# A two-layer graph attention kernel: one more slot in layer 1's ring of rows, no transfers for missing edges, another order of the tiles

## The chip, the core and the metric

The kernel runs on one core of one Trainium2 chip. A core has five engines with instruction streams of their own: TensorE (PE in the profile; its weight loads are PEld), VectorE (DVE), ScalarE (ACT), GpSimd (POOL) and SyncE (SP). SP and ACT issue plain DMAs. POOL issues the indirect ones, which read or write a row per partition at an index taken from memory. Sixteen DMA engines move the bytes of all of them. The metric is the time of one execution on the device in microseconds. Before the change the median of three runs is 5479.6 us (5479.25 to 5485.96).

## The reference

There are 10,000 nodes with 768 numbers each, 160,000 random directed edges (80,000 pairs, both ways) and 10,000 self-loops. A node has 17 incoming edges on average. Two graph attention layers follow each other, cut here to what matters:

```python
def gat_conv(x, W, a_src, a_dst, bias, heads, out_ch, concat):
    xl = (x @ W).reshape(n, heads, out_ch)
    alpha_src, alpha_dst = einsum(xl, a_src), einsum(xl, a_dst)     # one number per node and head
    e = leaky_relu(alpha_src[src] + alpha_dst[dst], 0.2)
    e = exp(e - segment_max(e, dst)[dst])
    alpha = e / (segment_sum(e, dst)[dst] + 1e-16)
    return segment_sum(xl[src] * alpha, dst) + bias                  # the sum over a node's edges

h = gat_conv(x, W1, ..., heads=4, out_ch=256, concat=True)           # 1024 numbers a node
h = relu(layer_norm(h)) + (x @ Wr1 + br1)
h1 = h
h = gat_conv(h, W2, ..., heads=1, out_ch=768, concat=False)          # 768 numbers a node
h = layer_norm(h) + (h1 @ Wr2 + br2)
out = layer_norm(x + h)
```

## The kernel before

**Tables.** For each layer the kernel writes a table with a row per node: the transformed features, then the node's source and destination logits. A row of `table1` has 1,033 numbers (4,132 bytes): 1,024 features, 4 source and 4 destination logits, and the node's rank (below) in the last column. A row of `table2` has 770 numbers (3,080 bytes). Both tables have a row more, number `NP`, for missing edges: its features are 0 and its logits are -1e30, so that its weight comes out as 0; in `table1` its rank is `NP` itself.

**First stage** (lines 591 to 660). A loop over the 79 tiles of 128 nodes computes `x @ W1` on PE and the logits on DVE and ACT, adds the bias on POOL and writes `table1`. Beside it `prepare` (line 188) finds each node's edges and sorts the nodes by degree: the rank is a node's place in that order. Tile `t` of the sorted nodes gets `SLOTS[t]` slots, a bound on the degree of its nodes: 41 for tile 0, 27, 26, 25, 24, 24 for the next, 17 for tiles 36 to 43, 9 for tile 77 and 8 for tile 78; 1,377 in all. `slots` holds, for each partition and slot, the row to fetch; a slot without an edge holds `NP`. Slot 0 of a tile is the node's own row.

**The order of the tiles.** `TURNS` (line 96) gives the order in which both layers go through the tiles: 78, 76, ..., 2, 0, then 1, 3, ..., 77. So the numbers of slots rise from 8 to 41 and fall to 9.

**The ring** (`Ring`, line 434). A layer's gathered rows lie in a ring of `RING1` = 28 or `RING2` = 38 slots, 128 rows each. `ring.fetch` issues, on POOL, one indirect DMA per slot (line 418, through `gather`), in order; the gather of slot q + 28 is issued in the program after the work on slot q and waits for the engines that read it. In layer 2 a tile's own rows (slot 0) come by a plain DMA on SP instead, as the table lies in sorted order.

**Layer 1** (`ordered_layer1`, line 668). For each tile: `logits` (line 461) computes the weights of all its slots on DVE, with the exponential on ACT, and then copies the ranks from the last column of the fetched rows into `slots` (line 478, ACT), since layer 2's table lies in sorted order and its gathers need ranks. `normalised` divides the weights by their sum. The first one to four slots are added up on PE with diagonal matrices (lines 703 and 709). Of the others, each fourth is multiplied and added on DVE, head by head (line 508, four operations); the rest are multiplied by their weights on ACT (line 497) and added by DVE (line 504). Beside it PE transposes x and multiplies it by Wr1, and transposes the tile before, h, and multiplies it by W2. The weights of the next tile are begun when three slots of this one are left (`LEAD`), if `SLOTS[t + 1] + LEAD` is no more than the ring; so DVE then needs all rows of the next tile. A tile with more slots than the ring goes through `attend_parts` (line 511).

**x in layer 1.** `fetch_x` (line 677) gathers the tile's rows of x (384 KB) into one of two buffers. The rows of tile t + 2 are asked for at the end of tile t.

**Layer 2** (`ordered_layer2`, line 814) has the same shape with one head of 768: 512 columns are weighted on DVE (line 508), 256 on PE (line 860). PE also computes the residual (lines 871 and 874) from h1 and x. The result is scattered to the node's place by an indirect DMA on POOL with a bound (line 893): indices of nodes that don't exist are skipped.

```python
nc.gpsimd.indirect_dma_start(out=out, out_offset=bass.IndirectOffsetOnAxis(ap=nodes(t), axis=0),
                             in_=o, in_offset=None, bounds_check=N - 1, oob_is_err=False)
```

The order of the instructions on each engine is the order of the program (`tc.manual_schedule()`). `general_path` is for inputs that don't fit the slots; it doesn't run here.

Of the kernel before, what the change touches and what calls it, by code (L numbers as in the profile page):

```python
# [42 lines left out]
SCATTERS = 6  # L43
LISTS = 4
G = 4
RING1 = 28
RING2 = 38
LEAD = 3
DIAGONALS = 5
# [29 lines left out]
def gnn_kernel(ctx, tc, x, x_cols, src, dst, src_col, dst_col, W1, a_src1, a_dst1, b1, g1, be1, Wr1, br1,  # L79
               W2, a_src2, a_dst2, b2, g2, be2, Wr2, br2, out, n_edges):  # L80
    nc = tc.nc
    N, D0 = out.shape
    H1, DH1 = a_src1.shape
# [9 lines left out]
    CAPS = slot_counts(N, n_edges)  # L93
    SLOTS = CAPS

    TURNS = list(range(NT - 1, -1, -2))
    TURNS += sorted(set(range(NT)) - set(TURNS))
    FIRST, TOTAL = [0] * NT, 0
    for t in TURNS:
# [88 lines left out]
    def prepare():  # L188

        with tc.tile_pool(name="prep", bufs=1, side="right") as pool, \  # L190
# [107 lines left out]
                base, s = more, 2 * s  # L298
            nc.vector.tensor_sub(base, base, each)
            rank = pool.tile([P, NT], F32, name="rank")  # L300
            to = pool.tile([P, NT], I32, name="to")
            written = 0

# [33 lines left out]
            with nc.allow_non_contiguous_dma(reason="16 bytes a node"):  # L337
                for to, d in zip([sorted_] + others, order_d):
                    nc.sync.dma_start(to, d.rearrange("(t p) f -> p t f", p=P))
                    yield  # L340
                nc.sync.dma_start(table1[:NP, R1 - 1:].rearrange("(p j) r -> p (j r)", p=P), rank)
                yield
            for other in others:
                nc.vector.tensor_add(sorted_, sorted_, other)
# [72 lines left out]
    def gather(to, table, index, **more):  # L417
        nc.gpsimd.indirect_dma_start(out=to, out_offset=None, in_=table,  # L418
                                     in_offset=bass.IndirectOffsetOnAxis(ap=index, axis=0), **more)
# [14 lines left out]
    class Ring:  # L434

        def __init__(self, pool, table, row, size, own):
            self.table, self.size, self.own, self.issued = table, size, own, 0
            self.rows = pool.tile([P, size, row], F32, name="ring")  # L440

        def fetch(self, upto):
            for q in range(self.issued, min(upto, TOTAL)):
                if q in self.own:
                    nc.sync.dma_start(self.slot(q), self.table[self.own[q] * P:(self.own[q] + 1) * P, :])
                else:
                    gather(self.slot(q), self.table[:, :], slots[:, q:q + 1])
                self.issued = q + 1

        def slot(self, q):  # L450
# [10 lines left out]
    def logits(small, ring, lo, hi, ad, heads, c, top=None):  # L461


        n = hi - lo
        e = small.tile([P, ring.size, heads], F32, name="e")[:, :n]
        for a, b, rows in ring.parts(lo, hi):
            nc.vector.tensor_tensor(e[:, a - lo:b - lo], rows[:, :, c:c + heads],
                                    ad[:, None, :].to_broadcast([P, b - a, heads]), op=OP.add)
        leaky(e, e)
        new = small.tile([P, heads], F32, name="new")  # L470
        nc.vector.reduce_max(new, e.rearrange("p k h -> p h k"), axis=AX.X)
        if top is not None:
            nc.vector.tensor_max(new, new, top)
        nc.vector.tensor_tensor(e, e, new[:, None, :].to_broadcast([P, n, heads]), op=OP.subtract)  # L474
        nc.scalar.activation(e, e, AF.Exp)  # L475
        if not ring.own:
            for a, b, rows in ring.parts(lo, hi):
                nc.scalar.copy(slots[:, a:b], rows[:, :, R1 - 1])
        return e, new

    def normalised(small, e, heads, t):
# [109 lines left out]
    with tc.tile_pool(name="w1", bufs=1) as w1p, tc.tile_pool(name="l1", bufs=2) as io, \  # L591
# [14 lines left out]
        none = w1p.tile([P, R1], F32, name="none")[:1]  # L606
        nc.vector.memset(none[:, :C1], 0.0)
        nc.vector.memset(none[:, C1:], -BIG)
        nc.vector.memset(none[:, R1 - 1:], float(NP))
        nc.scalar.dma_start(table1[NP:NP + 1, :], none)  # L610
        nc.scalar.dma_start(table2[NP:NP + 1, :], none[:, C1 - C2:C1 + 2 * H2])

# [4 lines left out]
        def weight_steps():  # L617

            with nc.allow_non_contiguous_dma(reason="1024 numbers"):
                nc.scalar.dma_start(br1_c, br1.rearrange("(k p) -> p k", p=P))
            yield
            yield
            brT = spread_br1(w1p, "brT")
            load(w2, W2)
            for i, a in enumerate((a_src2, a_dst2)):
                vec = spread(w1p, a, "a2")
                for k in range(K1):
                    yield  # L630
                    m = io.tile([P, C1], F32, name="scr")[:, :C2]
                    nc.vector.tensor_mul(m, w2[:, k, :C2], vec)
                    nc.scalar.activation(m, m, AF.Copy, accum_out=w2[:, k, C2 + i:C2 + i + 1])
            load(wr1, Wr1)
            yield
            q = product(brT, w2, R2)
            row = io.tile([P, R1], F32, name="row")
            nc.scalar.copy(row[:, :R2], q[:, :R2])
            nc.vector.tensor_add(lift, row[:, C2:C2 + 1], row[:, C2 + 1:R2])
            nc.scalar.dma_start(shift, row[0:1, :C2])  # L640
# [3 lines left out]
        for t in range(NT):  # L644
            p = product(xTs.pop(t), w1, C1)
            row = io.tile([P, R1], F32, name="row")
            nc.scalar.copy(row[:, :C1], p[:, :C1])  # L647
            for i, vec in enumerate((as_b, ad_b)):
                m = io.tile([P, C1], F32, name="scr")
                nc.vector.tensor_mul(m, p[:, :C1], vec)  # L650
                for h in range(H1):
                    s = slice(h * DH1, (h + 1) * DH1)
                    nc.scalar.activation(m[:, s], m[:, s], AF.Copy,
                                         accum_out=row[:, C1 + i * H1 + h:C1 + i * H1 + h + 1])
            nc.gpsimd.tensor_add(row[:, :C1], row[:, :C1], b1_b)  # L655
            load_x(t + 2)
            nc.sync.dma_start(table1[t * P:(t + 1) * P, :R1 - 1], row[:, :R1 - 1])
            next(steps, None)
# [9 lines left out]
    def ordered_layer1():  # L668
        nonlocal ps_big
        with tc.tile_pool(name="b1", bufs=1) as pool, tc.tile_pool(name="small1", bufs=2) as small, \  # L670
# [4 lines left out]
            ring.fetch(SLOTS[0])  # L675

            def fetch_x(t):
                xt = pool.tile([P, D0], F32, name="xt", bufs=2)
                gather(xt, x[:, :], nodes(t))
                return xt  # L680

            xs = {t: fetch_x(t) for t in range(min(2, NT))}
            ring.fetch(RING1)
            g1_b, be1_b = (spread(pool, v, n) for v, n in ((g1, "g1"), (be1, "be1")))

# [5 lines left out]
            def weights_of(t):  # L691

                n, m = SLOTS[t], on_pe(t)
                e, _ = logits(small, ring, FIRST[t], FIRST[t] + n, ring.slot(FIRST[t])[:, C1 + H1:C1 + 2 * H1], H1, C1)
                yield e
                normalised(small, e, H1, t)

# [34 lines left out]
            for t in range(NT + 1):  # L732
# [24 lines left out]
                moves = []  # L757
                if live:
                    xT = pool.tile([P, K0, P], F32, name="xT")
                    moves = columns(xT, xs[t])  # L760
                multiplied(first + 2)
                if last:
                    h = pool.tile([P, C1], F32, name="h")
# [16 lines left out]
                if last:  # L780
                    events.append((first + 2, to_layer2))

                def due(k):
                    while events and events[0][0] <= k:
                        events.pop(0)[1]()

                if live and not whole:
                    due(n)
                    acc = ps_acc.tile([P, 2 * BANK], F32, name="acc")
                    ad = small.tile([P, H1], F32, name="ad")  # L790
                    nc.vector.tensor_copy(ad, ring.slot(FIRST[t])[:, C1 + H1:C1 + 2 * H1])
                    attend_parts(small, ring, acc, acc, ad, None, H1, DH1, t)
                ready = []
                ahead = iter(())
# [12 lines left out]
                last = None  # L807
                if live:
                    last = r, acc
                    if t + 2 < NT:  # L810
                        xs[t + 2] = fetch_x(t + 2)
            store(NT - 1)

    def ordered_layer2():
        nonlocal ps_big
        with tc.tile_pool(name="b2", bufs=1) as pool, tc.tile_pool(name="small2", bufs=2) as small, \
# [28 lines left out]
            def weights_of(t):  # L845
# [1 line left out]

                n = SLOTS[t]
                ad = small.tile([P, H2], F32, name="ad")
                nc.vector.tensor_add(ad, ring.slot(FIRST[t])[:, C2 + H2:], lift)  # L850
# [53 lines left out]
            for t in range(NT):  # L904
# [4 lines left out]
                if not whole(t):  # L909
                    for _ in last:  # L910
                        pass
                    ad = small.tile([P, H2], F32, name="ad")
                    nc.vector.tensor_add(ad, ring.slot(FIRST[t])[:, C2 + H2:], lift)
# [34 lines left out]
    def general_path():  # L948
# [82 lines left out]
        def attend_chunks(keep, work, small, lists, table, row, heads, dh, t):  # L1031
# [7 lines left out]
            nc.vector.tensor_copy(top, acc[:, c:c + heads])  # L1039
# [3 lines left out]
            nc.vector.tensor_copy(adm[:, :heads], acc[:, c + heads:c + 2 * heads])  # L1043
# [7 lines left out]
            with tc.For_i(lo, hi, G) as i:  # L1051
# [19 lines left out]
                for g in range(0, G, zg):  # L1071
                    z = work.tile([P, zg, heads, P], F32, name="z")
                    nc.vector.tensor_tensor(
                        z, off[:, g:g + zg, None, :].to_broadcast([P, zg, heads, P]),
                        xg[:, g:g + zg, c:c + heads, None].to_broadcast([P, zg, heads, P]), op=OP.add)
# [22 lines left out]
                nc.vector.tensor_add(e, xg[:, :, c:c + heads], sel[:, :, :heads])  # L1098
# [118 lines left out]
```

## Time and profile before

| what | value |
|---|---|
| median of three runs | 5479.6 us |
| the profiled execution | 5488.77 us, span 5487.0 us, mean granted clock 0.938 |
| PE, PEld | 4754.0 us (87%), 2827.1 us (52%) |
| DVE | 4328.8 us (79%) |
| ACT | 3148.0 us (57%) |
| POOL | 3247.4 us (59%) |
| DMA | 1581.74 MB, mean 288 GB/s |
| ring gathers, both layers (L418) | 2,675, mean 969 ns on POOL |

The first layer's gathers begin at 905 us and the second layer's at 3488 us. Times in the profile are in us unless ns is said. A line of the timeline gives the start, the length, the engine, the line of the kernel, the operation, what it writes and reads, and in brackets how long the engine had stood idle before it and what ended that. A busy share is a mean over stages that have different limits, so each stage is looked at by itself.

### The profile page before, as it was taken

The page shows a single profiled execution, that of the slowest core. Times are in us where ns is not written, and L with a number is a line of the kernel's source. Part 1 is how long each engine was busy: PE and PEld are TensorE (multiplying, and loading weights), DVE is VectorE, ACT ScalarE, POOL GpSimd, SP SyncE. Part 2 cuts the span into 40 slices and gives each one's busy share as a digit, 9 for nine tenths or more (in the row PEclk, how much of TensorE's full clock was granted, in tenths as well). Part 3 has the DMA queues.
Part 4 walks back from the last instruction along what each step waited for, and adds up shares of the span by engine and source line. Part 5 has one row for each costly group of instructions (what it writes and reads, how often), then busy time and mean ns, then how long its engine had stood idle before and what let it go on. Part 6 is the DMA issues. An engine that isn't in the chain of part 4 may idle for free. (4 is left out here: it accounts for less than half of the span.)

```text
span 5487.0 us, 58297 instructions
## 1 busy us (share of the span) xinstructions
PE 4754.0 (87%) x15032; PEld 2827.1 (52%) x15032; DVE 4328.8 (79%) x7766; ACT 3148.0 (57%) x8255; POOL 3247.4 (59%) x3238
## 2 busy tenths in 40 slices
PE   8999997999999875478999999799988746888998
PEld 3444443555555543245555555466655524555665
DVE  5784244899998888788999999498877786778998
ACT  3433344788888877678888888244433312333444
POOL 2445455455566555455665554377777775777774
PEclk9999998999999988789999999899998877899999
DMA  4333625899999988789999997699999987999996
GB/s 152 124 95 82 94 91 202 316 328 339 339 361 347 344 303 301 285 315 345 353 359 347 341 329 263 239 340 360 345 333 321 336 297 258 331 323 349 349 355 240
DMA packets 457866, 1581.74 MB, mean 288 GB/s; under 512 B 111851, under 2 KB 116011, under 8 KB 457526
## 3 DMA queue, kind: packets, MB, share of 16 engines
q0 software_dynamic: 328704, 1339.21, 68.3%
q1 hardware_dynamic: 126768, 235.29, 13.1%
q10 hardware_dynamic: 2054, 3.42, 0.2%
q8 instruction: 126, 2.06, 0.2%
q14 instruction: 214, 1.75, 0.1%
HBM read 1431.80 MB, written 146.23 MB: 288 GB/s over the span
## 5 line engine op out<-in xcount | busy, mean ns | idle before, releaser
L418 POOL DMA_INDIRECT ring<-table,slots x2675 | 2591.7, 969 | 1635.6 <-DVE acc L508 402.4
L508 DVE SCALAR_TENSOR_TENSOR acc<-ring,e,acc 128x256 f32<-128x256 f32 (+1 forms) x2538 | 1572.0, 619 | 127.5 <-PE acc L709 52.0
L497 ACT ACTIVATE ring<-ring,e 128x256 f32<-128x256 f32 x3320 | 1351.0, 505 | 0.0
L504 DVE TENSOR_TENSOR acc<-acc,ring 128x1024 f32<-128x1024 f32 x830 | 1022.5, 1232 | 72.8 <-ACT ring L497 1.2
L874 PE MATMUL big<-wr,w 128*128 128x512 f32 (+1 forms) x2528 | 857.9, 493 | 0.0
L169 PE MATMUL big<-w,xT 128*128 128x512 f32 x1896 | 827.7, 598 | 28.9 <-DMA w<-in_W_dram 11.2
L169 PE MATMUL big<-wr,xT 128*128 128x512 f32 x1896 | 834.1, 596 | 0.7 <-ACT xT L575 0.7
L169 PE MATMUL big<-w,hT 128*128 128x512 f32 (+1 forms) x2528 | 832.1, 486 | 1.2 <-ACT hT L575 1.2
L860 PE MATMUL big<-ring,diagonals 128*128 128x256 f32 x2672 | 660.8, 409 | 185.3 <-ACT diagonals L859 177.0
L860 PEld LDWEIGHTS big<-ring,diagonals 128*128 128x128 f32 x2672 | 543.6, 206 | 299.4 <-ACT diagonals L859 201.2
L169 PEld LDWEIGHTS big<-w,hT 128*128 128x128 f32 x2528 | 478.4, 189 | 375.0 <-issue 341.3
L709 PE MATMUL acc<-ring,diagonals 128*128 128x256 f32 x1816 | 456.6, 409 | 247.9 <-ACT diagonals L703 216.5
L874 PEld LDWEIGHTS big<-wr,w 128*128 128x128 f32 x2528 | 488.1, 193 | 350.3 <-issue 317.7
L169 PEld LDWEIGHTS big<-w,xT 128*128 128x128 f32 x1896 | 362.7, 192 | 491.9 <-issue 472.8
L169 PEld LDWEIGHTS big<-wr,xT 128*128 128x128 f32 x1896 | 356.9, 192 | 421.2 <-issue 420.3
L709 PEld LDWEIGHTS acc<-ring,diagonals 128*128 128x128 f32 x1816 | 370.1, 206 | 326.8 <-ACT diagonals L703 235.7
L859 ACT ACTIVATE diagonals<-ident,e 128x128 f32<-128x128 f32 x1336 | 399.6, 387 | 155.6 <-DVE e L488 117.9
L554 ACT ACTIVATE sd<-mv,eps 128x1 f32<-128x1 f32 x237 | 69.8, 294 | 614.0 <-DVE mv L552 613.6
L650 DVE TENSOR_TENSOR scr<-big,as_b 128x1024 f32<-128x1024 f32 x79 | 96.8, 1225 | 391.9 <-ACT row L647 391.9
L655 POOL TENSOR_TENSOR row<-row,none 128x1024 f32<-128x1024 f32 x79 | 187.2, 2369 | 280.5 <-ACT row L647 279.9
L703 ACT ACTIVATE diagonals<-ident,e 128x128 f32<-128x128 f32 x908 | 278.5, 387 | 96.4 <-DVE e L488 96.4
L475 ACT ACT_TABLE_LOAD x153 | 196.3, 1283 | 233.1 <-DVE e L474 205.9
(172 smaller groups left out, 3895.5 us busy)
## 6 DMA issues: line engine op xcount, KB each, us to landing
ring<-table,slots POOLq DMA_INDIRECT x2675, 6.5
table<-row SPq DMA_DIRECT2D x79, 516.0 KB, 3.6
h_d<-hT SPq DMA_DIRECT2D x79, 512.0 KB, 7.2
w<-h_d SPq DMA_DIRECT2D x79, 512.0 KB, 8.4
table<-row SPq DMA_DIRECT2D x79, 385.0 KB, 6.2
ring<-table SPq DMA_DIRECT2D x79, 385.0 KB, 6.5
xT<-in_x_cols_dram SPq DMA_DIRECT2D x79, 384.0 KB, 4.5
wr<-in_Wr_dram SPq DMA_DIRECT2D x2, 3072.0 KB
```

Source lines behind the costliest of these rows:

```text
L169: nc.tensor.matmul(p[:, c:e], aT[:, j, :], w[:, j, c:e], start=(j == 0), stop=(j == k - 1))
L418: nc.gpsimd.indirect_dma_start(out=to, out_offset=None, in_=table, in_offset=bass.IndirectOffsetOnAxis(ap=index, axis=0), **more)
L475: nc.scalar.activation(e, e, AF.Exp)
L497: nc.scalar.activation(row[:, s], row[:, s], AF.Copy, scale=e[:, h:h + 1])
L504: nc.vector.tensor_add(acc[:, :c], acc[:, :c], row[:, :c])
L508: nc.vector.scalar_tensor_tensor(acc[:, s], row[:, s], e[:, h:h + 1], (acc if first is None else first)[:, s], op0=OP.mult, op1=OP.add)
L655: nc.gpsimd.tensor_add(row[:, :C1], row[:, :C1], b1_b)
L703: nc.scalar.activation(diagonals[:, k * H1 + i, :], ident, AF.Copy, scale=e[:, k, i:i + 1])
L709: nc.tensor.matmul(acc[:, c:d], diagonals[:, k * H1 + i, :], ring.slot(FIRST[t] + k)[:, c:d], start=(k == 0 and c % BANK == 0), stop=(k == ...
L859: nc.scalar.activation(diagonals[:, k % G, :], ident, AF.Copy, scale=e[:, k, :])
L860: nc.tensor.matmul(to, diagonals[:, k % G, :], ring.slot(FIRST[t] + k)[:, ON_PE2:C2], start=False, stop=(k == n - 1), skip_group_check=True)
L874: nc.tensor.matmul(r[:, c:d], hT[:, j, :], wr2[:, j, c:d], start=False, stop=(j == K1 - 1 and (d < C2 or not whole(t))), skip_group_check= ...
```

## The change

Four things change.

1. `RING1` is 29 instead of 28. x in layer 1 has one buffer instead of two; the gather of tile t + 1's x is issued in the course of tile t, after two slots past those on PE, instead of x of tile t + 2 at the end of tile t.
2. Gathers from the second turn of the ring on carry `bounds_check=NP - 1`: an index of `NP` fetches nothing, and the slot keeps what was there. So that what was there has no weight, `logits` now writes -1e30 into the source logits of the slots that it has just read. For this the two kinds of logits change places in the tables' rows, destination first, and `table1` holds the negated rank in its last column: the same memset covers it, and `slots` becomes the smaller of the negated column and `NP`.
3. The copy of the ranks into `slots` moves from ACT to DVE, as that multiplication with minimum; the memset is on DVE as well, in both layers.
4. `TURNS` is 78, 77, ..., 48, then 47, 45, ..., 1, then 0, 2, ..., 46. The numbers of slots are 8 to 16 in the first 31 tiles, rise to 41 and fall to 16.

```diff
-RING1 = 28
+RING1 = 29
-    TURNS = list(range(NT - 1, -1, -2))
+    TURNS = list(range(NT - 1, NT * 3 // 5, -1)) + list(range(NT * 3 // 5, -1, -2))
     TURNS += sorted(set(range(NT)) - set(TURNS))
...
-                nc.sync.dma_start(table1[:NP, R1 - 1:].rearrange("(p j) r -> p (j r)", p=P), rank)
+                nc.vector.tensor_scalar(less_rank, rank, -1.0, None, op0=OP.mult)
+                nc.sync.dma_start(table1[:NP, R1 - 1:].rearrange("(p j) r -> p (j r)", p=P), less_rank)
...
                 if q in self.own:
                     nc.sync.dma_start(self.slot(q), self.table[self.own[q] * P:(self.own[q] + 1) * P, :])
+                elif q < self.size:
+                    gather(self.slot(q), self.table[:, :], slots[:, q:q + 1])
                 else:
-                    gather(self.slot(q), self.table[:, :], slots[:, q:q + 1])
+                    gather(self.slot(q), self.table[:, :], slots[:, q:q + 1], bounds_check=NP - 1,
+                           oob_is_err=False)
...
-            nc.vector.tensor_tensor(e[:, a - lo:b - lo], rows[:, :, c:c + heads],
+            nc.vector.tensor_tensor(e[:, a - lo:b - lo], rows[:, :, c + heads:c + 2 * heads],
                                     ad[:, None, :].to_broadcast([P, b - a, heads]), op=OP.add)
...
         nc.scalar.activation(e, e, AF.Exp)
-        if not ring.own:
-            for a, b, rows in ring.parts(lo, hi):
-                nc.scalar.copy(slots[:, a:b], rows[:, :, R1 - 1])
+        for a, b, rows in ring.parts(lo, hi):
+            if not ring.own:
+                nc.vector.tensor_scalar(slots[:, a:b], rows[:, :, R1 - 1], -1.0, float(NP), op0=OP.mult, op1=OP.min)
+            nc.vector.memset(rows[:, :, c + heads:], -BIG)
         return e, new
...
             def fetch_x(t):
-                xt = pool.tile([P, D0], F32, name="xt", bufs=2)
+                xt = pool.tile([P, D0], F32, name="xt")
                 gather(xt, x[:, :], nodes(t))
                 return xt
 
-            xs = {t: fetch_x(t) for t in range(min(2, NT))}
+            xt = fetch_x(0)
             ring.fetch(RING1)
...
+                def next_x():
+                    nonlocal xt
+                    xt = fetch_x(t + 1)
+
+                if t + 1 < NT:
+                    events.append((first + 2, next_x))
...
                     last = r, acc
-                    if t + 2 < NT:
-                        xs[t + 2] = fetch_x(t + 2)
```

More of the change, by code (lines that the diff above doesn't have):

```diff
@@ L300, in prepare @@
             rank = pool.tile([P, NT], F32, name="rank")
+            less_rank = pool.tile([P, NT], F32, name="less_rank")
             to = pool.tile([P, NT], I32, name="to")
@@ L608, in gnn_kernel @@
         nc.vector.memset(none[:, C1:], -BIG)
-        nc.vector.memset(none[:, R1 - 1:], float(NP))
         nc.scalar.dma_start(table1[NP:NP + 1, :], none)
@@ L626, in weight_steps @@
             load(w2, W2)
-            for i, a in enumerate((a_src2, a_dst2)):
+            for i, a in enumerate((a_dst2, a_src2)):
                 vec = spread(w1p, a, "a2")
@@ L647, in gnn_kernel @@
             nc.scalar.copy(row[:, :C1], p[:, :C1])
-            for i, vec in enumerate((as_b, ad_b)):
+            for i, vec in enumerate((ad_b, as_b)):
                 m = io.tile([P, C1], F32, name="scr")
@@ L693, in weights_of @@
                 n, m = SLOTS[t], on_pe(t)
-                e, _ = logits(small, ring, FIRST[t], FIRST[t] + n, ring.slot(FIRST[t])[:, C1 + H1:C1 + 2 * H1], H1, C1)
+                e, _ = logits(small, ring, FIRST[t], FIRST[t] + n, ring.slot(FIRST[t])[:, C1:C1 + H1], H1, C1)
                 yield e
@@ L759, in ordered_layer1 @@
                     xT = pool.tile([P, K0, P], F32, name="xT")
-                    moves = columns(xT, xs[t])
+                    moves = columns(xT, xt)
                 multiplied(first + 2)
@@ L790, in ordered_layer1 @@
                     ad = small.tile([P, H1], F32, name="ad")
-                    nc.vector.tensor_copy(ad, ring.slot(FIRST[t])[:, C1 + H1:C1 + 2 * H1])
+                    nc.vector.tensor_copy(ad, ring.slot(FIRST[t])[:, C1:C1 + H1])
                     attend_parts(small, ring, acc, acc, ad, None, H1, DH1, t)
@@ L849, in weights_of @@
                 ad = small.tile([P, H2], F32, name="ad")
-                nc.vector.tensor_add(ad, ring.slot(FIRST[t])[:, C2 + H2:], lift)
+                nc.vector.tensor_add(ad, ring.slot(FIRST[t])[:, C2:C2 + H2], lift)
                 e, _ = logits(small, ring, FIRST[t], FIRST[t] + n, ad, H2, C2)
@@ L912, in ordered_layer2 @@
                     ad = small.tile([P, H2], F32, name="ad")
-                    nc.vector.tensor_add(ad, ring.slot(FIRST[t])[:, C2 + H2:], lift)
+                    nc.vector.tensor_add(ad, ring.slot(FIRST[t])[:, C2:C2 + H2], lift)
                     attend_parts(small, ring, h, h, ad, b2_b, H2, DH2, t)
@@ L1038, in attend_chunks @@
             top = keep.tile([P, heads], F32, name="top")
-            nc.vector.tensor_copy(top, acc[:, c:c + heads])
+            nc.vector.tensor_copy(top, acc[:, c + heads:c + 2 * heads])
             total = keep.tile([P, heads], F32, name="total")
@@ L1042, in attend_chunks @@
             adm = keep.tile([P, 2 * heads], F32, name="adm")
-            nc.vector.tensor_copy(adm[:, :heads], acc[:, c + heads:c + 2 * heads])
+            nc.vector.tensor_copy(adm[:, :heads], acc[:, c:c + heads])
             tmp = small.tile([P, heads], F32, name="tmp")
@@ L1074, in attend_chunks @@
                         z, off[:, g:g + zg, None, :].to_broadcast([P, zg, heads, P]),
-                        xg[:, g:g + zg, c:c + heads, None].to_broadcast([P, zg, heads, P]), op=OP.add)
+                        xg[:, g:g + zg, c + heads:c + 2 * heads, None].to_broadcast([P, zg, heads, P]), op=OP.add)
                     pz = ps_tr.tile([P, BANK // P, P], F32, name="tr")
@@ L1097, in attend_chunks @@
                 e = small.tile([P, G, heads], F32, name="ge")
-                nc.vector.tensor_add(e, xg[:, :, c:c + heads], sel[:, :, :heads])
+                nc.vector.tensor_add(e, xg[:, :, c + heads:c + 2 * heads], sel[:, :, :heads])
                 leaky(e, e)
```

## The prediction

> **What bounds the kernel now.** I read the busy times by stretch first, to find the stages and what is full in each; then, in each stage, the timeline of the engine that could be its bound; then the page's groups for durations. Columns of the first fence: stretch, its length, busy us and count of PE, PEld, DVE, ACT and POOL, granted clock, share of the DMA engines, GB/s.
>
> ```profile
> 1326.00:1354.00 28.00, 27.60 (x94) 16.62 (x94) 25.70 (x42) 23.28 (x59) 15.73 (x18) 1.00 0.96 352
> 2012.70:2057.10 44.40, 31.37 (x102) 19.26 (x101) 34.44 (x51) 32.97 (x85) 23.46 (x25) 0.85 0.83 303
> 4010.00:4440.00 430.00, 346.41 (x1168) 241.81 (x1169) 334.27 (x663) 157.37 (x401) 307.33 (x320) 0.88 0.92 325
> 5010.00:5428.00 418.00, 393.10 (x1356) 256.70 (x1355) 378.97 (x811) 181.94 (x435) 318.07 (x329) 0.97 0.97 355
> ```
>
> Every stage shows nearly full DMA engines, which invites the reading "bound by bytes". The timelines say otherwise. Layer 1 (905 to 3488 us), a tile of 24 rows followed by another; DVE:
>
> ```profile
> 2038.50 0.17 DVE L467 TENSOR_TENSOR e<-ring 128x16 f32<-128x16 f32 x1
> 2044.66 0.24 DVE L467 TENSOR_TENSOR e<-ring 128x80 f32<-128x80 f32 x1 [6.00 <-DMA ring<-table,slots]
> 2045.59 0.26 DVE L474 TENSOR_TENSOR e<-e,new 128x96 f32<-128x96 f32 x1
> 2045.76 2.06 DVE L508 SCALAR_TENSOR_TENSOR acc<-ring,e,acc 128x256 f32<-128x256 f32 x4
> ```
>
> DVE stands 6 us waiting for the next tile's last row, which could be issued only when a slot of the 28 came free. From one L765 to the next a tile of 13 or 14 rows takes 26, of 15 or 16 rows 28.3, of 17 29.7, of 18 30.2, of 19 31 to 32 us, with DVE at 0.92 and 30 ns between dependent operations: there DVE (with PE just behind; PE alone for 12 rows and fewer, 25.1 us) is the bound, not DMA. One more row should cost one L504, 1.27 us, or four L508, 2.06. Tiles of 20 to 24 rows take 34 to 48: more than that by the ring stall.
>
> Layer 2 (3488 to the end), POOL:
>
> ```profile
> 5128.23 0.95 POOL L418 DMA_INDIRECT ring<-table,slots  x1 [0.30 <-DVE acc L508]
> 5129.48 0.95 POOL L418 DMA_INDIRECT w<-in_x_dram,order  x1 [0.30 <-DMA ring<-table,slots]
> 5130.73 1.01 POOL L893 DMA_INDIRECT out_dram<-out,order  x1 [0.30 <-issue]
> 5132.05 0.97 POOL L418 DMA_INDIRECT ring<-table,slots  x1 [0.30 <-PE big L860]
> 5133.32 0.95 POOL L418 DMA_INDIRECT ring<-table,slots  x1 [0.30 <-PE big L860]
> ```
>
> POOL issues without a pause: 0.95 us and a fixed 0.30 between. A tile of n rows has n-1 gathers, one x gather and one scatter, (n+1) x 1.25 us: 20.0, 21.25 and 22.5 for 15, 16 and 17 rows, where the distance between scatters is 20.1 to 20.7, 21.4 and 22.6. So for 15 rows and more POOL's issue sets layer 2; for 14 and fewer PE does (12.8 us for residual and bias, L871, L874, L855, and 0.45 a row, L860: 18.6 us against POOL's 17.5 for 13 rows). Between 4010 and 5010 POOL also stands some 70 us for ring slots (19 rows and more).
>
> **The change part by part.** Base: the profiled execution, 5488.8 us (span 5487.0), 9.2 above the median of 5479.6.
>
> *Rows for missing edges.* From the inputs about 6,100 of 176,256 slots have no edge: 1,642 in tile 0, some 820 in tile 78 (among the first gathers, still fetched), the rest mostly whole slots, the last of a tile. The instructions stay; some 5,100 rows of 4,132 B and 5,000 of 3,080 B are not moved. Where DVE or POOL is the bound this is worth nothing. It is worth something only where the last row gates: in layer 1 the tiles 21, 15, 11, 7, 5, 3, 1, 2 lose (nearly) all of theirs, and one gather holds each DMA engine for 8 packets of 161 ns, 1.29 us: -10 us (0 to -14). In layer 2, nine such tiles by 8 x 120 ns: -9 (0 to -20). By bytes alone, at 345 GB/s, it would be -62 and -45; that is a rival below.
>
> The Trainium skill, "DMA: Bandwidth & Descriptors" (Anatomy of one DMA), calls descriptor generation small and puts a DMA at about 2.0 us fixed, overlappable, plus its bytes. By that the skipped bytes would be the whole story, an estimate of -85 us at the page's 436 GB/s. The POOL rows above speak against it here: issue spacing, not bytes, equals the tile time.
>
> *The check's price on POOL.* Every gather after the first ring now carries a bound. No checked gather is in the trace; the checked scatter L893 is:
>
> ```profile
> L893 POOL DMA_INDIRECT out_dram<-out,order x79: 982/1022/1688, 3563.5 to 5477.2; - x79
> L308 POOL DMA_INDIRECT order_d<-facts,to x79: 963/969/1003, 442.7 to 590.2; - x79
> 5468.21 0.98 POOL L893 DMA_INDIRECT out_dram<-out,order  x1 [10.92 <-ACT out L891]
> 5477.22 0.98 POOL L893 DMA_INDIRECT out_dram<-out,order  x1 [8.03 <-POOLq L1165]
> ```
>
> Between gathers it takes 1022 ns, 76 over their 946 and 53 over the unchecked scatter; but scatters that follow each other at the end take 982, 13 over L308, and the gather just after a scatter also loses 29. So most of the 53 looks like switching of kind, and like against like is 13 ns. I take 13; the ends are 0 and 76. It counts where POOL is the bound: tiles of 15 rows and more have 1,132 rows less 59 own rows; those of 19 and more (614) I count at 0.8: 950 x 13 ns = +12 us (0 to +72). In layer 1 POOL has 0.4 us and more to spare per row: nothing while that holds.
>
> *A 29th slot.* The time above the DVE work, by the NEXT tile's rows:
>
> ```
> rows of next tile   19    20    21    22    23    24
> excess us          0.8   1.9   3.2  4.25   5.7   7.3
> ```
>
> About 1.3 us per row, as the gating row is issued 26 - n' rows ahead (n' the next tile's rows); one more slot is one step to the left: 19 tiles with 20 or more x 1.3, 7 with 19 x 0.5, and the middle (tiles 1, 0, 2) 2: -30 us (-18 to -36). When it goes, the wait for the row remains the next latest thing until n' = 20.
>
> *x in mid-tile.* One xt: its gather waits for the transposes of the old one. In PE's order these come 1.7 us after the tile's first matmuls, before DVE's first weighing, so POOL and the ring gathers behind it don't stand; x is issued some 9 us into a tile of 25 to 30 and lands in 5 to 9. That cover fails once: at the start x of the second tile moves from tenth to thirty-fifth gather. At 1.25 us each from 904.96, it is issued at 947.5 and lands some 9.6 later, at 957, where PE now transposes at 944.4 and waits for h until 949.85:
>
> ```profile
> 944.39 0.82 PE L572 MATMUL big<-ident,xt 128*128 128x128 f32 x6
> 949.85 1.94 PE L572 MATMUL big<-ident,h 128*128 128x128 f32 x8 [4.64 <-DVE h L765]
> 951.58 12.16 PE L169 MATMUL big<-wr,xT 128*128 128x512 f32 x24
> ```
>
> The first tiles are PE's, so +8 us (0 to +9).
>
> *DVE's new operations.* 125 pairs (a multiply-and-min into slots, a memset that waits for it) in layer 1, 116 memsets in layer 2, for 126 copies on ACT, which was not the bound. By dependent operations of that size a pair is 0.17 + 0.24 + 0.06 = 0.47, 1.6 pairs a tile. They stand behind the exp, where DVE waits 0.52 us in most tiles:
>
> ```profile
> 1342.05 1.23 DVE L504 TENSOR_TENSOR acc<-acc,ring 128x1024 f32<-128x1024 f32 x1
> 1343.80 0.23 DVE L491 TENSOR_SCALAR e<-e,loops 128x4 f32<-128x4 f32 x1 [0.52 <-ACT e L475]
> ```
>
> What is left, 0.15 us of about 55 tiles: +8 (0 to +59, if that wait were no cover). Layer 2: POOL's time covers them but in the stalls, +3 (0 to +23).
>
> *The order.* Small tiles are all at the start. The sums over tiles are the same in both layers; in layer 2 POOL idles some 17 us more behind PE at the start and the drain after the last gather shrinks from 50 to about 36: +3 (-10 to +10). Negating rank and swapping the two columns: 0, hidden in the first stage beside PE's 10 us products.
>
> Sum: -10 - 9 + 12 - 30 + 8 + 8 + 3 + 3 = -15: 5473.8 against 5488.8, 5465 against the median.
>
> **The rivals.** (a) The check costs what the scatter shows, 53 to 76 ns a gather: +50 to +72 in place of +12, so 5503 to 5525, slower. It decides above 30 ns (950 x 17 more eats the 15). For: the 1022 and the 975 after it. Against: the 982s. (b) Bytes bind: -107 in place of -19, 5377, or up to 5400 where a stage keeps its own bound. For: DMA shares of 0.96; against: (n+1) x 1.25. (c) DVE gets no cover in layer 1: +51, 5516. Against: 40.7 us in 70 such waits. (d) The parts cancel: the ring gains its low end and the check 25 ns: 5476 to 5488.
>
> **How the numbers follow.** Less than 0.2% (11 us) is about what a measurement of this kernel can't tell from nothing. Likeliest case 0.55, with its own range 5440 to 5490 (0.36 faster, 0.14 same, 0.05 slower); (a) 0.20, (c) 0.06, both slower; (b) 0.12, faster; (d) 0.07, same. Faster 0.48, same 0.21, slower 0.31. The range 5425 to 5520 leaves out (b) and the end of (a).
>
> **What would show it.** Gathers of layer 2 at 0.96 and 1.26 apart (rival a: 1.00 and 1.30); DVE's waits for rows in layer 1's large tiles shorter by 1.3 us each; layer 1 shorter by about 24 us, layer 2 longer by about 9; PE's second xt transposes near 957; the wait before L491 gone. Wrong if spacing passes 1.28, if tiles of 13 to 18 rows in layer 1 grow, or if tiles of 15 to 17 rows in layer 2 go below (n+1) x 1.25.

## The result and the profile after

The changed kernel takes 5511.6 us (median of six runs, 5508.4 to 5523.8) where the kernel before takes 5484.0 beside it: a ratio of 1.006 (95% interval 1.0049 to 1.0071), slower by some 28 to 33 us. The forecast was 5465; 5511.6 lies in its range and in that of rival (a), 5503 to 5525.

Times below are cut at the first ring gather of each layer. "Layer 1" runs from its first gather to layer 2's first, "layer 2" from there to the end.

| stage | before | after | difference | predicted |
|---|---|---|---|---|
| up to layer 1's first gather | 904.96 | 895.32 | -9.6 | 0 |
| layer 1 | 2582.9 | 2561.1 | -21.8 | -24 |
| layer 2 | 1999.1 | 2050.9 | +51.7 | +9 |
| span | 5487.0 | 5507.3 | +20.3 | -15 |

The rows are of the two profiled executions, which lie 20.3 us apart where the medians lie 27.6. The first stage's 9.6 us are not of the change's making: next to nothing of it lies there, and three later runs of the same kernel took 903.6, 901.4 and 903.8 us for it. So layer 1's total came out near the predicted one, and layer 2 lost 43 us more than predicted.

Layer 2 after, the timeline of POOL among tiles of 15 and 16 rows (start, length, engine, line, operation, idle time before it and what ended that):

```profile
4011.47 0.98 POOL L421 DMA_INDIRECT w<-in_x_dram,order  x1 [0.30 <-DVE mv L560]
4012.75 1.03 POOL L905 DMA_INDIRECT out_dram<-out,order  x1 [0.30 <-issue]
4014.08 1.03 POOL L421 DMA_INDIRECT ring<-table,slots  x1 [0.30 <-DMA ring<-table,slots]
4015.41 1.00 POOL L421 DMA_INDIRECT ring<-table,slots  x1 [0.31 <-issue]
4016.72 1.00 POOL L421 DMA_INDIRECT ring<-table,slots  x1 [0.30 <-DVE ring L486]
```

A gather now takes 1.00 us and follows the last at 1.30; before it was 0.95 and 1.25. The pause of 0.30 is the same. The next two fences are from the lists of one line's instructions, of before and of after (count, then shortest/median/longest ns, then the start of the first and of the last):

```profile
L418 POOL DMA_INDIRECT ring<-table,slots x2675: 932/942/1957, 905.0 to 5425.8; - x192
L893 POOLq MOVE  x79: 29/29/29, 3557.8 to 5468.0; - x79
```

```profile
L421 POOL DMA_INDIRECT ring<-table,slots x2675: 937/995/2033, 895.3 to 5455.6; - x192
L421 POOLq MOVE  x2612: 29/29/29, 930.8 to 5448.8; - x187
```

All gathers of both layers are in these rows. Split by layer, the median of a gather was 936 ns in layer 1 and 946 in layer 2 before; with a bound it is 992 and 1002. Some 4 ns of that is the profile's: in after, the gathers of each ring's first turn, which have no bound, take 941 and 949. So the bound costs 51 to 53 ns a gather, and the same comes out within every other profile that has both kinds. Each of the 2,612 gathers that has one also got a `MOVE` of 29 ns on POOL's sequencer. The bounded scatter L893 had the same `MOVE` in the profile before, and neither the unbounded gathers nor the unbounded scatter L308 had one: a sign that stood there to be read.

Layer 1 after, DVE at the place that was shown of before, the end of a tile of 23 rows whose next has 24 (so it was before, too, where the prediction speaks of a tile of 24 rows followed by another):

```profile
2426.98 0.25 DVE L474 TENSOR_TENSOR e<-ring 128x92 f32<-128x92 f32 x1 [3.09 <-DMA ring<-table,slots]
...
2428.09 0.36 DVE L485 TENSOR_SCALAR slots<-ring 128x1 int32<-128x1 f32 x2
2428.31 0.39 DVE L486 MEMSET ring<- 128x5 f32 x2
2428.62 1.98 DVE L516 SCALAR_TENSOR_TENSOR acc<-ring,e,acc 128x256 f32<-128x256 f32 x4
2430.51 0.22 DVE L499 TENSOR_SCALAR e<-e,loops 128x4 f32<-128x4 f32 x1
```

The wait for the last row is 3.09 us where it was 6.00. The new operations (L485, L486) stand where DVE used to wait for the exponential, and the bracket ahead of L499 is gone. The list of layer 1's waits says the same of the whole layer (us in total, times, longest). Before:

```profile
DVE e L467 <- DMA ring<-table,slots: 63.5, 23, 24.4
...
DVE e L491 <- ACT e L475: 37.7, 67, 2.7
DVE e L467 <- issue: 18.0, 7, 4.3
```

After:

```profile
DVE e L474 <- DMA xt<-in_x_dram,order: 24.4, 1, 24.4
DVE e L474 <- DMA ring<-table,slots: 23.7, 12, 4.1
DVE acc L512 <- ACT ring L505: 11.6, 6, 9.5
DVE e L499 <- ACT e L482: 7.9, 11, 2.3
...
DVE e L474 <- issue: 0.2, 1, 0.2
```

The one wait of 24.4 us is the start of the layer in both. Without it DVE's waits ahead of the logits, those for which no releaser is shown included, went from 57.1 us to 23.9, and those for the exponential from 37.7 to 7.9. The 9.5 us in the third row are one wait, in the second tile, at the place where x comes late.

The price of the single x buffer is on PE, in that second tile:

```profile
932.27 1.89 PE L716 MATMUL acc<-ring,diagonals 128*128 128x256 f32 x8
947.36 1.51 PE L580 MATMUL big<-ident,xt 128*128 128x128 f32 x6 [13.20 <-DMA xt<-in_x_dram,order]
```

PE takes x 52.0 us after the layer's first gather, which is what was worked out (957 less 904.96), and the tile, of 9 rows, is 31.0 us long where the second tile, of 10 rows, was 22.1.

### The profile page after: what moved, and what is told of

It reads as the page before. It is cut to its first block, busy times and chain, and to the rows that moved or that the text cites. A ratio compares the mean times of both kernels' runs of the same rounds, so it can differ in the third digit from the quotient of the medians.

```text
span 5507.3 us, 60788 instructions
## 1 busy us (share of the span) xinstructions
PE 4745.0 (86%) x15032; PEld 2818.9 (51%) x15032; DVE 4355.2 (79%) x8127; ACT 3134.4 (57%) x8125; POOL 3393.1 (62%) x3238
## 5 line engine op out<-in xcount | busy, mean ns | idle before, releaser
L421 POOL DMA_INDIRECT ring<-table,slots x2675 | 2734.1, 1022 | 1524.3 <-issue 369.7
L872 PE MATMUL big<-ring,diagonals 128*128 128x256 f32 x2672 | 656.6, 407 | 186.4 <-ACT diagonals L871 171.2
L872 PEld LDWEIGHTS big<-ring,diagonals 128*128 128x128 f32 x2672 | 540.7, 205 | 298.9 <-ACT diagonals L871 203.3
L657 DVE TENSOR_TENSOR scr<-big,ad_b 128x1024 f32<-128x1024 f32 x79 | 96.7, 1224 | 385.5 <-ACT row L654 385.5
L660 ACT ACTIVATE scr<-scr 128x256 f32<-128x256 f32 x632 | 253.6, 403 | 123.0 <-DVE scr L657 123.0
```

Of the source, the lines that this page charges most:

```text
L660: nc.scalar.activation(m[:, s], m[:, s], AF.Copy, accum_out=row[:, C1 + i * H1 + h:C1 + i * H1 + h + 1])
L872: nc.tensor.matmul(to, diagonals[:, k % G, :], ring.slot(FIRST[t] + k)[:, ON_PE2:C2], start=False, stop=(k == n - 1), skip_group_check=True)
```

## The experiments

The theory after the result: the bound costs POOL some 55 ns a gather (the figure of the expectations, before the 4 ns of the profile were taken off), and since POOL paces layer 2 most of that is on the path. Rivals: the new order of tiles or the new operations lengthen layer 2; or layer 2 waits for bytes.

The chips of these runs are of two kinds, which has to be known to read them. On those of the result and of the first runs (**A**; "fast" in the expectations) the kernel before takes 5484 and 5476 us. On the four of the later runs (**B**; "slow" in the expectations) it takes 5788 to 5829, nearly all of the difference in layer 2. Each chip stands for one occasion only, so whether it is the chip or the occasion that differs is not shown. Each ratio is to the kernel before on the same chip.

| run | what it is | kind | ratio to before (95%) | layer 1 | layer 2 |
|---|---|---|---|---|---|
| before | | A | 1 | 2582.9 | 1999.1 |
| after | | A | 1.006 (1.0049 to 1.0071) | 2561.1 | 2050.9 |
| before_bound | only the bound | A | 1.0075 (1.0058 to 1.0092) | 2579.2 | 2042.1 |
| l2_unchecked | after, no bound in layer 2 | A | 0.9993 (0.9984 to 1.0003) | 2560.5 | 2014.3 |
| after_old_order | after, old order | A | 1.0022 (1.0012 to 1.0031) | 2548.1 | 2041.7 |
| l2_no_rows | after, layer 2's rows not moved | A | 5477.5 us, one run | 2563.5 | 2016.9 |
| before_ring29 | only slot and x | B | 0.9943 (0.9922 to 0.9964) | 2558.4 | 2293.6 |
| before_new_order | only the order | B | 1.0006 (0.9996 to 1.0017) | 2598.9 | 2293.0 |

On B layer 1's first result comes 55 to 57 us after its first gather instead of 42 to 44, whatever the kernel; layer 1 of A and B is compared with these 13 us taken off, or by sums over the same tiles.

### The bound alone

```diff
-                    gather(self.slot(q), self.table[:, :], slots[:, q:q + 1])
+                    gather(self.slot(q), self.table[:, :], slots[:, q:q + 1], bounds_check=NP, oob_is_err=False)
```

> The kernel before, with a bound on every gather that no index exceeds: every row is fetched as before, and only the comparison is added. Theory: layer 2's gathers 1.00 us long and 1.30 us apart, layer 2 longer by 45 to 60 us, layer 1 within 5 us of before since POOL has slack there: 5530 to 5545 us. Rival (a bound costs some 13 ns, and layer 2's loss has another cause): 5484 to 5500 us.

Measured 5517.2 us, 41 above the kernel before beside it (5476.0): less than the 5530 to 5545 expected (which were reckoned from 5484, not 5476), clearly outside the rival's 5484 to 5500. Layer 1 is 3.7 us shorter than before's, so no cost there; layer 2 is 43.0 longer. Its POOL:

```profile
5131.73 0.99 POOL L418 DMA_INDIRECT ring<-table,slots  x1 [0.31 <-issue]
5133.03 1.00 POOL L418 DMA_INDIRECT ring<-table,slots  x1 [0.30 <-issue]
```

No index exceeds this bound and every row is fetched. The price is that of having a bound, not of skipping. 43.0 us by 52 ns are 830 of layer 2's 1,298 ring gathers.

### The bound taken out of layer 2

```diff
-                elif q < self.size:
+                elif q < self.size or self.own:
```

> The kernel after, with layer 2's gathers without a bound (a missing edge's row is fetched again); layer 1, the order of tiles and the memsets stay. Theory (the bound costs POOL 55 ns a gather, and POOL paces layer 2): gathers of layer 2 back at 0.95 us and 1.25 us apart, layer 2 shorter by 45 to 55 us, 5456 to 5467 us in all, below the kernel before (5484). Rival (the new order of tiles or the memsets in front of layer 2's exp lengthen it): 5500 to 5512 us, layer 2 within 10 us of 2050.9.

Measured 5473.2 us, far from the rival and somewhat above the theory: layer 2 gives back 36.6 of its 51.7, not 45 to 55. It is not back to before (2014.3 against 1999.1), so the bound is not the whole of it. By 52 ns these are 700 gathers. Where the rest went is seen in the whole of layer 2, without the bound and with it (stretch, length, busy us and count of PE, PEld, DVE, ACT, POOL, granted clock, share of the DMA engines, GB/s):

```profile
3459.01:5473.29 2014.28, 1658.36 (x5704) 1117.62 (x5704) 1617.61 (x3449) 740.97 (x1810) 1420.44 (x1456) 0.91 0.90 323
3456.44:5507.31 2050.87, 1666.87 (x5704) 1117.83 (x5704) 1617.37 (x3449) 739.95 (x1810) 1493.88 (x1456) 0.90 0.88 309
```

POOL is busy 73.4 us more for the same 1,456 instructions, and layer 2 is 36.6 longer: half of the added time came out of POOL's idle time, which fell from 593.8 to 557.0 us.

### Layer 2 without its bytes

```diff
-                    gather(self.slot(q), self.table[:, :], slots[:, q:q + 1], bounds_check=NP - 1,
+                    gather(self.slot(q), self.table[:, :], slots[:, q:q + 1], bounds_check=0 if self.own else NP - 1,
```

> The kernel after, with the bound of layer 2's gathers lowered to 0, so that they move the row of node 0 alone and leave out all others (which leaves out layer 2's data, not its instructions). Theory (POOL's issue paces layer 2, not bytes): tiles of 15 to 17 rows stay at (n+1) x 1.30 us, 20.9 to 23.5 us; stalls for late rows in tiles of 19 rows and more shrink; 5460 to 5510 us. Rival (layer 2 waits for bytes): its tiles go down to PE's 18 to 20 us, 5300 to 5400 us.

With this bound layer 2's gathers past the ring's first turn move the row of node 0 alone. Measured 5477.5 us, once. The same stretch of layer 2, tiles of 12 to 16 rows, in after, in this run and in l2_unchecked (columns as above):

```profile
3650.00:4140.00 490.00, 463.76 (x1628) 305.41 (x1627) 424.97 (x958) 207.98 (x496) 377.31 (x370) 0.99 0.94 336
```

```profile
3650.00:4140.00 490.00, 467.99 (x1643) 308.19 (x1642) 427.39 (x962) 207.70 (x495) 377.13 (x371) 0.99 0.28 84
```

```profile
3650.00:4140.00 490.00, 474.37 (x1683) 314.74 (x1682) 438.45 (x982) 214.21 (x503) 372.53 (x382) 0.99 0.97 355
```

With a quarter of the bytes POOL gets through 371 instructions in the 490 us where after gets through 370: DMA engines that go from 0.94 busy to 0.28 change nothing here. Without the bound it gets through 382, with more bytes, not fewer. Over the whole of layer 2 the bytes are worth 34 us (2050.9 to 2016.9), mostly in tiles of 18 rows and more (-29 over 36 tiles) and next to nothing in the 23 tiles of 15 to 17 rows (494.6 to 490.7). The rival of bytes is out for tiles of 12 to 17 rows on this kind of chip; in the larger ones late rows do hold layer 2 up. The Trainium skill, "DMA: Bandwidth & Descriptors" (Anatomy of one DMA), calls the generation of descriptors small and its cost late to show; here 1.30 us of POOL a gather is what these tiles take, and the measurement decides.

### The order of the tiles

```diff
-    TURNS = list(range(NT - 1, NT * 3 // 5, -1)) + list(range(NT * 3 // 5, -1, -2))
+    TURNS = list(range(NT - 1, -1, -2))
```

> The kernel after, with the order of tiles of the kernel before, the rest as it is. Theory: the order is worth little, within 15 us of the kernel after: 5497 to 5525 us. Rival (the order causes layer 2's loss): 5450 to 5480 us.

Measured 5488.2 us, 1.0022, inside the band that was given, but with 0.0038 less than after's 1.006 the order is worth about 21 us, where the prediction had 3. Layer 1 is 13.1 shorter than with the new order and layer 2 9.2. Since the two ratios come from two chips, the pair was run on one:

> The kernel after, to stand beside the next two on one chip. On a chip where before takes 5470 to 5490: ratio 1.004 to 1.007. On one where it takes 5790: 0.990 to 0.992.

> The kernel after with the old order, beside the kernel after. Theory: on a fast chip 15 to 25 us below the kernel after; on a slow one within 10 us of it (the new order alone gave 1.0006 there). Rival (the 1.0022 of the first run was that chip's): within 8 us on a fast chip too.

On B: 0.9925 (0.9896 to 0.9954) and 0.9885 (0.9857 to 0.9912), medians 5782.7 and 5761.5: 21 us again, 15.3 of it in layer 1 and 7.3 in layer 2. The theory's "within 10 us" on this kind missed. The order by itself, the new line put into the kernel before:

> The kernel before with the order of tiles of the kernel after, nothing else. Theory from the kernel after with the old order: layer 1 longer by 5 to 13 us (the small tiles next to each other and next to the late start), layer 2 by 5 to 10: 10 to 22 us slower, ratio 1.002 to 1.004. The prediction's term: +3 us (-10 to +10), ratio 0.998 to 1.002.

1.0006 (0.9996 to 1.0017): some 3 us, the prediction's number, and not the 10 to 22 that the runs above suggested. So the order is cheap in the kernel before and dear in the kernel after. Sums over the same tiles of layer 1 (us) show a part of it:

| rows of a tile | before (A) | before_new_order (B) | after_old_order (A) | after (A) |
|---|---|---|---|---|
| 9 to 12, 8 tiles | 192.7 | 200.9 | 203.8 | 212.5 |
| 13 to 17, 34 tiles | 953.3 | 955.8 | 955.2 | 953.5 |
| 18 to 21, 24 tiles | 792.6 | 797.8 | 774.4 | 773.5 |
| 22 to 41, 12 tiles | 573.4 | 567.8 | 546.8 | 557.1 |

Small tiles one after another cost 8 us in either kernel. In the large tiles the new order gains 5.6 us with 28 slots and loses 10.3 with 29. The two runs of after and of the old order on one chip of kind B show the same, 10.4 and 6.9 us lost. Why it turns round there is not settled. In layer 2, tiles of 9 to 12 rows take 138.6 us in after and 119.4 with the old order, part of which a shorter end gives back: 50.7 us from the last gather to the end against 61.6.

### Slot and x alone

```diff
-RING1 = 28
+RING1 = 29
-                xt = pool.tile([P, D0], F32, name="xt", bufs=2)
+                xt = pool.tile([P, D0], F32, name="xt")
...
+                if t + 1 < NT:
+                    events.append((first + 2, next_x))
```

> The kernel before with 29 slots in layer 1's ring and one x buffer fetched in mid-tile; no bound, the old order, the old copies on ScalarE. Theory of the prediction (slot -30, late second x +8): layer 1 some 22 us shorter, 5450 to 5460 us. Rival (the slot is worth all that layer 1 gained under the old order, 35 us, and the rows left out nothing): 5438 to 5446 us. Layer 2 within 5 us of before in either.

> The kernel before with 29 slots and one x buffer in mid-tile, on this chip. On the last chip layer 1 of this kernel was 2558.4 us and that of the kernel after 2570.5 in the new order (2582.9 for before on the first chip). Theory: slot and x alone give 22 to 30 us, ratio 0.9945 to 0.996, layer 2 unchanged. Rival (the rows left out carry part of layer 1's gain): under 15 us, ratio over 0.997.

Both fell on chips of kind B, so the times that were expected can't be held against the 5761.3 and 5760.1 measured; the ratios can: 0.9943 (0.9922 to 0.9964) and 0.9944 (0.9926 to 0.9962), some 33 us. Over the tiles of 18 rows and more the kernel before takes 1366.0 us, this one 1329.5 and 1329.1, after_old_order 1321.2 and its second run, on B, 1325.3. So the slot is worth some 36.5 us and the rows left out, with the new operations of DVE, 4 to 8. The late x doesn't show here: on B the whole start is late, and the second tile covers it (192.5 to 193.3 us for tiles of 9 to 12 rows, against 203.8 in after_old_order on A).

### The bound on the other kind of chip

> The kernel after, unchanged, on the chip of these runs, so that its parts are compared on one chip. Theory (check and order share layer 2's loss: the kernel after less the bound in layer 2 gave 5473, less the new order 5488): 5500 to 5512 us, so that the bound is worth 30 to 40 us and the order 12 to 24. Rival (the chips differ by more than the parts): under 5495.

> The kernel after once more, since the last chip gave 5796 us for the kernel before, with PE standing some 300 us in layer 2 for nothing that the profile shows, where the chips of the first runs gave 5476 to 5484. Theory (where POOL paces layer 2, the bound costs 37 to 43 us and the new order some 20): ratio to before 1.004 to 1.007 on a chip where before takes 5470 to 5490; below 1 on one like the last. Rival (the first verdict was that chip's alone): ratio under 1.002 on any chip.

The kernel after, unedited, on two chips of kind B, where the times expected first could not come: 0.9916 (0.9897 to 0.9934) and 0.9907 (0.9887 to 0.9927). It is faster there. Theory and rival of the second text both put it there on such a chip, so this decides nothing between them. That the loss was the first chip's alone is answered by before_bound and l2_unchecked, which show the bound's price on the next occasion of kind A; the kernel after itself was not run there.

> The kernel after without the bound on layer 2's gathers, beside the kernel after. Theory: on a fast chip, where POOL paces layer 2, 33 to 43 us below the kernel after; on a slow one, where PE and ScalarE stand for other reasons and POOL has slack, the bound is worth under 15 us and the rows fetched again cost some 30: above the kernel after or equal. Rival (the bound costs the same wherever it is run): 33 to 43 us below on either kind.

Beside after_fourth (5782.7) the kernel without the bound in layer 2 takes 5796.1, with intervals that overlap (0.9943, 0.9919 to 0.9967): the bound's 36.6 us are not there. Its price per gather is the same as on A. Layer 2 without the bound and with it, on this chip (l2_unchecked_again, after_fourth):

```profile
3473.46:5777.79 2304.33, 1776.99 (x5704) 1165.49 (x5704) 1621.08 (x3449) 754.66 (x1810) 1417.00 (x1456) 0.86 0.82 282
3469.28:5766.86 2297.58, 1776.53 (x5704) 1159.37 (x5704) 1620.79 (x3449) 749.84 (x1810) 1494.13 (x1456) 0.86 0.81 276
```

POOL is busy 77.1 us more, and all of it came out of its idle time. POOL's timeline in layer 2 of after_third shows what that idle time is:

```profile
3905.02 0.99 POOL L421 DMA_INDIRECT ring<-table,slots  x1 [2.20 <-PE big L872]
3906.32 1.00 POOL L421 DMA_INDIRECT ring<-table,slots  x1 [0.30 <-PE big L872]
...
3926.86 0.99 POOL L421 DMA_INDIRECT ring<-table,slots  x1 [2.49 <-PE big L872]
```

Gathers are 1.00 us long and 1.30 apart as on A, but every few rows POOL stands for a slot that PE still reads (L872). Of layer 2's 1,157 ring gathers that directly follow another on POOL, 107 come after a pause of over 0.4 us; in after on A it is 37. Where POOL waits for others, 52 ns more in its instruction are paid out of the wait. What holds PE up on these chips is open. The groups of that line (busy us, mean ns, idle before it and what ended most of that) of after on A and of after_third:

```profile
L872 PE MATMUL big<-ring,diagonals 128*128 128x256 f32 x2672 | 656.6, 407 | 186.4 <-ACT diagonals L871 171.2
```

```profile
L872 PE MATMUL big<-ring,diagonals 128*128 128x256 f32 x2672 | 739.2, 429 | 280.0 <-issue 220.0
```

On A PE waits for ACT's diagonals; on B it stands for nothing that the trace shows. These traces also lack the landings of DMAs, so a wait for bytes would look the same. Why after's layer 2 is shorter than the old code's there (2254.7 against 2293.6 in before_ring29 on one chip) is open too.

### Versions beyond the change

```diff
-                elif q < self.size:
+                elif q < self.size or self.own:
...
             xt = fetch_x(0)
+            early = None
+            if NT > 1:
+                early = pool.tile([P, C1], F32, name="h")[:, :D0]
+                gather(early, x[:, :], nodes(1))
...
-                    xt = fetch_x(t + 1)
+                    xt = fetch_x(t + 1) if t else early
```

> The kernel after with the old order, no bound and no memsets in layer 2, and x of the second tile fetched early into the buffer of h; x is still gathered in layer 2. Theory: only the gains of layer 1 are left, 35 to 45 us, layer 2 as before: ratio 0.991 to 0.995 on a chip where before takes 5470 to 5490, 0.988 to 0.994 on one where it takes 5790. Rival (something else in the change costs layer 2 time): 0.996 or more.

With that, the old order, and the memset of `logits` in layer 1 alone, best_a: on B 0.994 (0.992 to 0.996), layer 2 2303.8. It is no better there than after; on A it was not run.

Layer 2's x rows are the ones that layer 1 has already gathered. Keeping them takes one issue a tile off POOL:

```diff
+    x_d = dram.tile([NT, P, D0], F32, name="x_d")
...
-                gather(xt, x[:, :], nodes(t))
+                nc.sync.dma_start(xt, x_d[t])
                 return hT.rearrange("p (k n) -> p k n", n=P), xt
...
+                    nc.sync.dma_start(x_d[t], xs[t])
```

> The kernel before, but layer 1 also stores its gathered x rows (one SyncE transfer a tile to a buffer in DRAM), and layer 2 loads them from there by SyncE, so that GpSimd issues one gather less a tile. Bytes grow. Theory (POOL's issues, 1.25 us each, pace layer 2 for 15 rows and more; PE takes over at 15 and 16 rows): layer 2 shorter by 30 to 65 us, 5410 to 5446 us. Rival (layer 2 is held by bytes or by SyncE's queue): 5470 us or more.

On B: 0.983 (0.9805 to 0.9855), 109 us less, though 31 MB more are moved. Layer 2 is 2160.7 us against 2293.6 for the same layer 2 with the gather on that chip (before_ring29). That is 133 us or 1.68 a tile, twice what was expected and more than the 1.25 us of an issue, so POOL's issue alone does not explain it on this kind. Layer 1 pays: its tiles of 18 rows and more take 1378.2 us instead of the 1366.0 of before on A.

> A version from what is known: 29 slots, layer 1's bound and rows left out, the old order, layer 2's gathers without a bound and without memsets, x of the second tile fetched early into the buffer of h, and layer 2's x loaded by SyncE from a copy that layer 1 stores. Theory: layer 1 35 to 45 us shorter than before, layer 2 30 to 65 shorter: 5370 to 5412 us. Rival (the gains share one cover): 5420 to 5450 us.

> The combined version on this chip (29 slots, bound and left-out rows in layer 1 only, old order, second x early, layer 2's x from a copy by SyncE). Theory: layer 1 35 to 45 us shorter than before, layer 2 30 to 65 shorter: ratio 0.980 to 0.988. Rival (the gains share one cover): 0.990 or more.

> The combined version. On a fast chip layer 2 is shorter than before by 30 to 60 us and layer 1 by 15 to 30 (storing x cost layer 1 some 14 us in the tiles): ratio 0.984 to 0.992; on a slow one 0.975 again.

> The same with layer 2's x loaded by SyncE from the copy that layer 1 stores. Theory: one issue less a tile on POOL, 30 to 60 us less in layer 2, some 14 more in layer 1: 15 to 50 us below the version beside it on a fast chip; 60 to 110 on a slow one, where before with that change alone gained 109.

The two together came in four times, on four chips of kind B: 0.9749, 0.9754, 0.9722 and 0.9724, each to 0.003 or better. The times of the first expectation can't be compared; the second had put 0.980 to 0.988, the third 0.975 for such a chip. On each it beats the kernel before, and the kernel after on the three where that ran. On the last, beside best_a, it is 127 us shorter, where 60 to 110 was put; layer 2 is 2168.3 against 2303.8. It never fell on a chip of kind A, so what it gives there is not known.

## Why the prediction was wrong, step by step

- **Where the bound lies** (POOL in layer 2, DVE and the ring in layer 1): right on A. The bytes are ruled out by l2_no_rows for the tiles up to 17 rows, and (n+1) times the issue distance nearly holds with 1.30: 20.8 and 22.1 us for tiles of 15 and 16 rows, where 21.1 to 22.2 and 22.2 to 22.7 were measured.
- **The check's price on POOL** is the step that failed. It was taken as 13 ns, from scatters at the drain against scatters of the first stage; it is 52, and the distance of 1.30 us passes the 1.28 that the prediction had named as its sign of being wrong. What failed is the step from a scatter to a gather. The "switching of kind" that the prediction took out of the scatter's 53 is real: in layer 2 of before the scatter takes 1022 ns after a gather and 982 after a scatter, and in l2_no_rows the x gather, which has no bound, takes 973 after a bounded gather, where it takes 946 after an unbounded one in l2_unchecked. So that the 53 comes near the 52 is luck. The number of gathers that pay in full, 950, was too high: the cost is that of 700 to 830. (Its 614 rows should be 609, which changes nothing.) In place of +12 us the bound costs 37 to 43.
- **Rows left out**: 36.7 MB less were moved, as worked out. In layer 1, with DVE's operations, -4 to -8 where -10 and +8 were put. In layer 2, with the memsets, 0 (after_old_order 2041.7 against before_bound 2042.1) where -9 and +3 were.
- **The 29th slot**: some -36.5 where -30 was put, at the end of its span. The wait shown above is 2.9 us shorter; 1.3 of that was put for the slot and 1.29 for the row left out of tile 5, which stands at that place in the new order.
- **x in mid-tile**: +9.6 in the second tile (22.1 to 31.7 in after_old_order) where +8 was; right to the microsecond in when PE gets it.
- **DVE's new operations**: nothing in layer 1's tiles of 13 to 17 rows (953.3 to 953.5); the wait for the exponential covered them. By the prediction's own rows, 1.6 pairs of 0.47 us less 0.52, some 0.23 us a tile would have been left, not 0.15.
- **The order**: +3 was right for the kernel before and wrong for the kernel that has the other edits: 21 us, of which 9 in layer 2 by the mechanism named (POOL idle behind small tiles), and 13 in layer 1, where the text said that the sums don't change.

That layer 1 came out at -21.8 against -24 is luck: the slot and the rows left out gained more than was put, and the new order took it back. Layer 2's 51.7 are 43.0 of bound, about 0 of rows and memsets and 9.2 of order. Rival (a) named the mechanism; that its sum fits is in part luck too, with a bound worth less and an order that costs more than it said.

## What to carry to other kernels

Price an option of an instruction by that instruction with and without it; a sibling with the option at another place in the program carries that place's other differences, and an extra sequencer instruction in the profile is a sign that the option costs something. On an engine that issues nearly without a pause, a few tens of ns by a thousand issues reach the path as far as the engine has no idle time to take them from: here half of them on one kind of chip and none on the other. Leaving out the transfers themselves gives none of the engine's own time back. Edits that share a margin, here the ring's slots and the order of tiles, are not additive: the price of one is to be measured with the others in place.

## What was not expected of the hardware

- An indirect gather of 128 rows costs POOL the same whether it moves its rows or hardly any: 1.30 us from one to the next at 84 GB/s as at 336.
- A bound adds 52 ns to a gather, and a `MOVE` of 29 ns on the sequencer, though no index exceeds it. An unbounded gather just behind a bounded one takes 27 ns more than behind an unbounded one.
- The same program takes 5476 to 5484 us on the chips of the first runs and 5788 to 5829 on four others, and one change is 1.006 on the former and 0.991 to 0.993 on the latter: a ratio of this size holds for the kind of chip it was measured on.
